# Four chained graph layers on one core: norms in two parts with pinned relus, another product order between two layers, and one turn moved to TensorE

## The chip, the core and the metric

The kernel runs on one core of a Trainium2 chip. The metric is the device time of one launch in microseconds (us). Before the change the median of three runs is 2624.2 us, the lowest 2624.03 and the highest 2625.35.

A core has engines that each work through a queue of their own: TensorE (PE, matrix products and 128x128 transposes, with weight loads PEld beside them), VectorE (DVE), ScalarE (ACT), GpSimd (POOL) and SyncE (SP, which here only issues DMAs). Engines wait for each other by semaphores. PSUM has eight banks, in which TensorE leaves its products and from which DVE and ACT fetch them ("evict").

## The reference, cut to what matters

`x` is 128 graphs of 128 nodes with 256 features. Four layers follow each other. Each begins with a layer norm without gain and a relu, and adds its result to `x`.

```python
# layer 0: three gates per node, two mixings by adj
h = relu(layernorm(x)); x = x + gated_mix(h, adj, edge_bias, ...)
# layer 1: attention of each graph within itself, masked
h = relu(layernorm(x)); x = x + (softmax(q k^T / 16 + adj, causal) v) Wo
# layer 2: three products, each followed by a mixing by A2 = adj * adj
h = relu(layernorm(x))
h = relu(A2 @ (h @ W1)); h = relu(A2 @ (h @ W2)); x = x + A2 @ (h @ W3)     # 256->512->1024->256
# layer 3: A_hat mixing, linear, batch norm over all nodes of all graphs, relu, linear, batch norm
h = relu(layernorm(x)); x = x + batchnorm(relu(batchnorm(A_hat @ h @ bW1.T + b1)) @ bW2.T + b2)
```

The layer norm needs the mean and the variance of each row of 256 numbers. The batch norms need the mean over everything, so the kernel has two passes: the first does all up to the first batch norm and writes `z` and `x` to DRAM, the second does the rest. All arithmetic is in float32.

## The kernel before

Four graphs make a group; there are 32. In the first pass a loop over groups `g` weaves four strands: layer 0 of group g+2 ("A"), the end of layer 1 and beginning of layer 2 of group g+1 ("B", then "b" for its successor), W2 and W3 of layer 2 for group g ("C"), layer 3 of group g-1 ("D", then "d"). Each strand is a Python generator. A string says which strand records its next piece:

```python
TURN = "CCBBCBCABCBBCABDBACBDDACDCADDCDCBDCADBCBACACbCBCBBCBBCBBCBCbBCd"
FINAL = "CCCCCCCCCCCCCCCCCCDCCCCDDdDDddDdDdDDdddd"      # last group
...
for k in TURN if g < LAST else FINAL:
    next(stream[k], None)
```

The layer norm of a group: statistics on DVE, four small operations on POOL, four relus on ACT with scale and bias.

```python
def norm(g, layer, bs=ALL, blocks=False):
    ...
    for k, b in enumerate(bs):
        nc.vector.bn_stats(st[:, k, :], xt[:, b, :])          # L366
    for k in range(n):
        nc.vector.bn_aggr(mv[:, k, :], st[:, k, :])           # L368
    ...
        nc.gpsimd.tensor_scalar(rs, mv[:, :, 1], LN_EPS, None, ALU.add)       # L372
        nc.gpsimd.tensor_tensor(rs, rs, nhalf[:, :n], ALU.pow)                # L373
        nc.gpsimd.tensor_scalar(sh, mv[:, :, 0], -1.0, None, ALU.mult)        # L374
        nc.gpsimd.tensor_tensor(sh, sh, rs, ALU.mult)                         # L375
    ...
        relu = nc.scalar.activation(                                          # L387
            dst, src, AF.Relu, bias=sh[:, k : k + 1], scale=rs[:, k : k + 1])
        if (g, layer) == (1, 0):
            tc.keep_in_program_order(relu)
    return h
```

`keep_in_program_order` pins an instruction: the recording layer may move others on their engine, not this one.

Layer 1 needs `h` transposed. The first group does it on TensorE (`turn`: eight 128x128 transposes into two PSUM banks, one evicted by ACT, one by DVE). The others send `h` to DRAM and back so that 32x32 blocks come to stand in their places (`swap`: four DMAs out, one back), and DVE turns the blocks (`cut`, L435):

```python
    h = norm(g, 1, bs, n == G)
    if n == G:
        blocks = h.rearrange("p b d -> p (b d)")
        swap(blocks, f"hc_{g}")
    yield
    hT = tile_of(g, bs, [P, DC, T], "dT", f"hT_{g}", 2)
    if n < G:
        turn(hT, h, bs, f"pt_{tail}")
    else:
        cut(hT.rearrange("p c t -> p (c t)"), blocks, DC * G)
```

The gate weights of layer 0 are made by twelve DVE operations `gs<-h,gw` (L558) of a group, a small sum `gl` and a sigmoid on ACT (`gt`, L566). With `gt`, ACT and DVE then make the matrices `m` (L577, L578, L585) and the bias (L589, L592); `m` goes through DRAM as `cc` and is turned by DVE (L435) before the products `pm<-h,m` (L610).

Products of 2x2 blocks are done in seven multiplications (`seven`, a Strassen-Winograd form): its pieces are called x, y, z (r = 0, 1, 4), then 5, 2, 6, 3. Between them ACT keeps copies (`p_t<-p_x`, L506) and DVE adds them.

```python
    px = bank(...); product(0, px, True);  t1 = kept(px, 1);             yield
    py = bank(...); product(1, py, True);  put((0, 0), py, t1);          yield
    pz = bank(...); product(4, pz, True);  t5 = kept(pz, 5);             yield
    product(5, px, False); t2 = kept(px, 2);                             yield
    product(2, pz, False); put((0, 1), pz, t2);                          yield
    product(6, px, False); put((1, 1), px, t5);                          yield
    product(3, px, False); put((1, 0), px, None);                        yield
```

In layer 2 the W2 products are two such sevens (`wide(0)`, `wide(1)`), and W3 is a third. The last `put` of `wide(q)` relus on ACT (L795) and makes four sums `h2s` on DVE (L457 to L460), which W3's third and later pieces read.

```python
    yield from wide(0)
    late = wide(1)
    for _ in range(6):
        yield next(late)
    third = seven(rows_by_half(h2s, SETS["3"], P), put_s, [P, 2, P], f"p3_{g}")
    yield next(third)           # W3's first piece
    yield from late             # then the seventh of the second W2
    yield from third
```

Meanwhile group g+1 begins its layer 2: norm, mixing `pm<-a2T,h` (L446), eviction `mT<-pm` on DVE and ACT (L449), sums `ms`, then the seven products `pu` with W1 (L474).

Of the kernel before, what the change touches and what calls it, by code (L numbers as in the profile page):

```python
# [15 lines left out]
P = 128  # L16
# [6 lines left out]
def kernel(  # L23
# [328 lines left out]
    def tile_of(g, bs, shape, tag, name, bufs):  # L352

        if len(bs) == G:
            return w.tile(shape, FP, tag=tag, name=name, bufs=bufs)
        if name not in whole:
            whole[name] = w.tile(shape, FP, tag=tag, name=name, bufs=bufs)
        return whole[name]

    def norm(g, layer, bs=ALL, blocks=False):  # L360

        xt, n, tail = X[g], len(bs), f"{layer}_{g}_{bs[0]}"
        st = small.tile([P, n, 6], FP, tag="st", name=f"st{tail}")
        mv = small.tile([P, n, 2], FP, tag="mv", name=f"mv{tail}")
# [4 lines that stand above are left out]
        rs = small.tile([P, n], FP, tag="rs", name=f"rs{tail}")  # L369
        sh = small.tile([P, n], FP, tag="sh", name=f"sh{tail}")  # L370
# [5 lines that stand above are left out]
        else:  # L376
            inv_sqrt(rs, mv[:, :, 1], LN_EPS)
            nc.vector.scalar_tensor_tensor(sh, mv[:, :, 0], -1.0, rs, ALU.mult, ALU.mult)
        h = tile_of(g, bs, [P, G, D], "h", f"h{layer}_{g}", 3)
        for k, b in enumerate(bs):  # L380
            dst, src = h[:, b, :], xt[:, b, :]
            if blocks:
                dst = h.rearrange("p b d -> p (b d)").rearrange(
                    "p (j k b r) -> p b j k r", j=P // 32, k=DC, b=G
                )[:, b]
                src = src.rearrange("p (k j r) -> p j k r", k=DC, j=P // 32)
            relu = nc.scalar.activation(  # L387
                dst, src, AF.Relu, bias=sh[:, k : k + 1], scale=rs[:, k : k + 1]
            )
            if (g, layer) == (1, 0):  # L390

                tc.keep_in_program_order(relu)
        return h

    def columns(dst, c, bs):

# [137 lines left out]
    def layer0(g, bs=ALL):  # L534

        xt, n, tail = X[g], len(bs), f"{g}_{bs[0]}"
        h = norm(g, 0, bs)
        yield
        gl = small.tile([P, n, 3], FP, tag="gl", name=f"gl_{tail}")
        gate_bias = gb[:, None, :].to_broadcast([P, n, 3])  # L540
        if g < 2:

            hT = tile_of(g, bs, [P, DC, T], "dT", f"h0T_{g}", 2)
            turn(hT, h, bs, f"ph_{tail}")
            yield
            pl = bank([P, n, 3], f"pl_{tail}")
            for k, b in enumerate(bs):
                for c in range(DC):
                    nc.tensor.matmul(
                        pl[:, k, :], hT[:, c, b * P : (b + 1) * P], gwT[:, c, :],  # L550
                        start=(c == 0), stop=(c == DC - 1),
                    )
            nc.vector.tensor_tensor(gl, pl, gate_bias, ALU.add)
        else:
            gs = w.tile([P, D], FP, tag="gs", name=f"gs_{tail}", bufs=1)
            for k, b in enumerate(bs):
                for i in range(3):
                    nc.vector.scalar_tensor_tensor(  # L558
                        gs, h[:, b, :], 1.0, gw[:, i, :], ALU.mult, ALU.mult,
                        accum_out=gl[:, k, i : i + 1],  # L560
                    )
                if k == n // 2 - 1:
                    yield
            nc.vector.tensor_tensor(gl, gl, gate_bias, ALU.add)
        gt = small.tile([P, n, 3], FP, tag="gt", name=f"gt_{tail}")
        nc.scalar.activation(gt, gl, AF.Sigmoid)  # L566
        yield


        um = tile_of(g, bs, [P, 2, G, D], "um", f"m_{g}", 1)  # L570
        bias = um[:, 0]
        cmb, cmbT = (
            um[:, 1, 2 * k : 2 * k + 2, :].rearrange("p a (b n) -> p (a b) n", n=P) for k in range(2)
        )
        flatT = cmbT.rearrange("p b n -> p (b n)")
        for k, b in enumerate(bs):
            nc.scalar.activation(cmb[:, b, :], ain, AF.Copy, scale=gt[:, k, 0:1])  # L577
            nc.vector.scalar_tensor_tensor(  # L578
                cmb[:, b, :], aout, gt[:, k, 1:2], cmb[:, b, :], ALU.mult, ALU.add
            )  # L580
            dst, one, now = cmb[:, b, :], ident, cmb[:, b, :]
            if g >= 2:
                dst = flatT.rearrange("p (j b r) -> p b j r", j=NQ, b=G)[:, b]
                one, now = (a.rearrange("p (j r) -> p j r", j=NQ) for a in (one, now))
            nc.vector.scalar_tensor_tensor(dst, one, gt[:, k, 2:3], now, ALU.mult, ALU.add)  # L585
        if g >= 2:
            swap(flatT, f"cc_{g}")
        for k, b in enumerate(bs):
            nc.scalar.activation(bias[:, b, :], eb, AF.Copy, scale=gt[:, k, 0:1])  # L589
        yield  # L590
        for k, b in enumerate(bs):
            nc.vector.scalar_tensor_tensor(  # L592
                bias[:, b, :], oeb, gt[:, k, 1:2], bias[:, b, :], ALU.mult, ALU.add
            )
        mine = slice(bs[0], bs[-1] + 1)
        if g >= 2:
            yield
            cut(cmb.rearrange("p b n -> p (b n)"), flatT, G)
            cmbT = cmb
        else:  # L600
            pc = bank([P, n, P], f"pc_{tail}")
            for k, b in enumerate(bs):
                nc.tensor.transpose(pc[:, k, :], cmb[:, b, :], ident)
            nc.vector.tensor_copy(cmbT[:, mine, :], pc)
        yield
        for q in range(bs[0] // 2, (bs[-1] + 1) // 2):
            pm = bank([P, 2, D], f"pm_{g}_{q}")
            for r in range(2):
                b = 2 * q + r
                nc.tensor.matmul(pm[:, r, :], cmbT[:, b, :], h[:, b, :], start=True, stop=True)  # L610
            half = slice(2 * q, 2 * q + 2)
            nc.vector.tensor_tensor(bias[:, half, :], pm, bias[:, half, :], ALU.add)
        yield
        nc.vector.scalar_tensor_tensor(
            xt[:, mine, :], bias[:, mine, :], 0.0, xt[:, mine, :], ALU.max, ALU.add
        )
        yield

    def layer1(g, bs=ALL):
# [1 line left out]

        xt, n, tail = X[g], len(bs), f"{g}_{bs[0]}"
        halves = range(bs[0] // 2, (bs[-1] + 1) // 2)
        h = norm(g, 1, bs, n == G)
        if n == G:
            blocks = h.rearrange("p b d -> p (b d)")
            swap(blocks, f"hc_{g}")
        yield
        hT = tile_of(g, bs, [P, DC, T], "dT", f"hT_{g}", 2)
        if n < G:  # L630
            turn(hT, h, bs, f"pt_{tail}")
        else:
            cut(hT.rearrange("p c t -> p (c t)"), blocks, DC * G)
            yield
            ex = w.tile([P, 4, 1, T // 2], FP, tag="ex", name=f"hs_{g}", bufs=2)
            hs = sums(nc.vector, quarters_t(hT), ex, ex[:, 3])
# [99 lines left out]
                    ALU.mult, ALU.add,  # L736
                )
        yield
        h = norm(g, 2, bs)
        yield  # L740
        mT = tile_of(g, bs, [P, DC, T], "dT", f"mT_{g}", 2)
        mixed(mT, h, a2T, f"pm2_{tail}", (nc.vector.tensor_copy, nc.scalar.copy), bs)
# [37 lines left out]
    def layer2(g):  # L780
# [39 lines left out]

        yield from wide(0)
        late = wide(1)
        for _ in range(6):
            yield next(late)
        third = seven(rows_by_half(h2s, SETS["3"], P), put_s, [P, 2, P], f"p3_{g}")
        yield next(third)
        yield from late
        yield from third
        for q in range(G // 2):
            pr = bank([P, 2, D], f"pr_{g}_{q}")  # L830
# [7 lines left out]
    def layer3(g):  # L838
# [1 line left out]

        parts = [ALL] if g < LAST else HALVES
        for bs in parts:
            h = norm(g, 3, bs)
            yield
        gT = tile_of(g, parts[0], [P, DC, T], "dT", f"gT_{g}", 2)
        for i, bs in enumerate(parts):
# [57 lines left out]

    TURN = "CCBBCBCABCBBCABDBACBDDACDCADDCDCBDCADBCBACACbCBCBBCBBCBBCBCbBCd"


    FINAL = "CCCCCCCCCCCCCCCCCCDCCCCDDdDDddDdDdDDdddd"  # L910
    US = {}
    AHEAD = 3

# [23 lines left out]
    for g in range(NG):  # L937
        if g + AHEAD < NG:
            load_x(g + AHEAD)
        if g == LAST:  # L940
            most1 = bn_part(stats1, FC, slice(LAST - 1), "most1")
        stream = {
            "A": part(layer0, g + 2), "B": bs, "C": layer2(g), "D": ds,
            "b": part(layer1, g + 2), "d": layer3(g),
        }
        for k in TURN if g < LAST else FINAL:
            next(stream[k], None)
        assert all(next(stream[k], k) == k for k in "ABCD")
        bs, ds = stream["b"], stream["d"]
# [243 lines left out]
```

## Time and profile before

| | |
|---|---|
| median of three runs | 2624.2 us |
| span of the profiled run | 2625.7 us |
| PE busy | 2524.2 us, 96% |
| DVE, ACT, POOL busy | 74%, 48%, 10% |
| stage 1000 to 1500 us (seven groups): PE busy | 489.93 of 500 us |
| stage 0 to 130 us: PE busy | 50.28 and 53.17 of two times 65 us |
| stage 2350 to 2550 us (second pass): PE busy | 199.9 of 200 us |

To read it: busy time is a share of the span, and PE's is a mean over three stages. The first 130 us prepare weights and fill the strands; from then to about 2300 us a group takes 71.6 us (in the timeline, the products `pmu` of one group begin at 1002.87 us and those of the next at 1074.51); the second pass follows. A time in square brackets in a timeline row is how long the engine sat idle before the row, and what ended the wait. A timeline's row shows a duration that overlaps the next row of the same engine a little: the distance between starts is the pace.

### The profile page before, as it was taken

To read this page: it belongs to the slowest core of one execution; us is meant where nothing else is said; L and a number is where in the kernel's file an instruction comes from. 1 tells how busy PE (TensorE), PEld (TensorE's weight loads), DVE (VectorE), ACT (ScalarE), POOL (GpSimd) and SP (SyncE) were. 2 spreads that over 40 slices of the span, in tenths; PEclk is the share of its full clock that TensorE was granted. 3 is DMA by queue.
4 is the path that set the end of the run, shared out by engine and by line. 5 is a ranking of instruction groups with operands and counts; after the bars stand their busy time and mean duration, and the time that the engine had idled before them with its cause. 6 is when DMAs were issued, how large, how long until landed. Compare 5 with 4: busy or idle time off the path is not lost.

```text
span 2625.7 us, 40828 instructions
## 1 busy us (share of the span) xinstructions
PE 2524.2 (96%) x14824; PEld 2255.9 (86%) x14824; DVE 1934.7 (74%) x4795; ACT 1248.9 (48%) x2546; POOL 269.1 (10%) x563
## 2 busy tenths in 40 slices
PE   7899999999999999999999999999999999999996
PEld 6788888888888888888888888888888888888885
DVE  7677777777777877777777777777777777548886
ACT  4444444444444444444444444444444444337766
POOL 1100111110011100111110011100111110000000
PEclk9899999999999999999999999999999999999998
DMA  4122211221121122211221221122112211026559
GB/s 132 48 64 65 57 46 60 65 65 57 57 65 56 58 65 65 57 46 60 65 65 57 58 65 57 57 65 65 50 52 61 65 57 55 26 83 229 176 183 386
DMA packets 115900, 207.59 MB, mean 79 GB/s; under 512 B 11618, under 2 KB 77684, under 8 KB 111732
## 3 DMA queue, kind: packets, MB, share of 16 engines
q1 hardware_dynamic: 109124, 181.85, 22.2%
q0 software_dynamic: 6432, 23.07, 2.5%
q8 instruction: 117, 1.92, 0.3%
q14 instruction: 83, 0.68, 0.1%
q10 hardware_dynamic: 144, 0.07, 0.0%
HBM read 105.72 MB, written 99.22 MB: 78 GB/s over the span
## 4 chain that ended last, share of the span: by engine, by line
PE 52%; DVE 21%; issue 11%; ACT 10%; POOL 4%; DMA 0%; SPq 0%; DVEq 0%; ACTq 0%; POOLq 0%
PE p_x L491 9%; PE p_x L474 7%; ACT h L387 5%; PE p_z L491 5%; PE pu_x L474 4%; PE pmu L446 4%; DVE gs L558 4%; PE pz_x L491 4%; DVE st L366 3%; PE p_z L474 2%; PE p_y L491 2%; DVE h2T L802 2%; POOL rs L373 2%; PE py L731 2%; PE ps L691 2%
## 5 line engine op out<-in xcount | busy, mean ns | idle before, releaser
L387 ACT ACTIVATE h<-x,sh,rs 128x256 f32<-128x256 f32 x512 | 269.2, 590 | 266.1 <-POOL sh L375 248.4
L491 PE MATMUL p_x<-uT,w 128*128 128x256 f32 x1024 | 247.5, 380 | 0.0
L803 ACT ACTIVATE h2T<-h2T 128x512 f32<-128x512 f32 x192 | 120.4, 627 | 223.8 <-DVE h2T L802 223.8
L506 ACT COPY p_t<-p_x 128x512 f32<-128x512 f32 (+1 forms) x192 | 96.1, 501 | 274.4 <-PE p_x L491 272.2
L491 PEld LDWEIGHTS p_x<-uT,w 128*128 128x128 f32 x1024 | 192.6, 191 | 38.3 <-issue 14.6
L558 DVE SCALAR_TENSOR_TENSOR gs<-h,gw 128x256 f32<-128x256 f32 x360 | 152.3, 423 | 79.6 <-ACT h L387 64.2
L366 DVE BATCH_NORM_STATS2 st<-x 128x6 f32<-128x256 f32 x512 | 182.5, 411 | 1.2
L372 POOL TENSOR_SCALAR rs<-mv 128x4 f32<-128x4 f32 x124 | 29.7, 240 | 1328.3 <-DVE mv L368 1275.6
L373 POOL TENSOR_TENSOR rs<-rs,nhalf 128x4 f32<-128x4 f32 x124 | 128.5, 1037 | 0.0
L491 PE MATMUL p_z<-us,w 128*128 128x256 f32 x512 | 125.3, 388 | 2.0 <-ACT p_t L506 1.9
L474 PEld LDWEIGHTS p_x<-w,h2T 128*128 128x128 f32 x1024 | 124.3, 192 | 3.3
L491 PE MATMUL p_z<-us,w_s 128*128 128x256 f32 x512 | 126.9, 382 | 0.0
L474 PE MATMUL p_x<-w,h2T 128*128 128x128 f32 x1024 | 124.6, 275 | 0.0
L491 PE MATMUL p_x<-uT,w_s 128*128 128x256 f32 x512 | 121.7, 380 | 1.3 <-DVE h2T L802 1.3
L491 PE MATMUL p_x<-us,w_s 128*128 128x256 f32 x512 | 121.0, 379 | 0.0
L491 PE MATMUL p_y<-uT,w 128*128 128x256 f32 x512 | 120.9, 379 | 0.0
L446 PE MATMUL pmu<-a2T,u 128*128 128x128 f32 x1024 | 119.6, 275 | 0.0
L446 PEld LDWEIGHTS pmu<-a2T,u 128*128 128x128 f32 x1024 | 116.9, 192 | 0.0
L449 DVE COPY uT<-pmu 128x512 f32<-128x512 f32 (+1 forms) x132 | 88.2, 672 | 36.6 <-PE pmu L446 36.4
L491 PEld LDWEIGHTS p_z<-us,w 128*128 128x128 f32 x512 | 95.2, 191 | 17.9 <-ACT p_t L506 2.6
L756 ACT ACTIVATE u<-u 128x512 f32<-128x512 f32 x93 | 58.6, 630 | 107.6 <-DVE u L755 106.5
L491 PEld LDWEIGHTS p_y<-uT,w 128*128 128x128 f32 x512 | 97.3, 190 | 13.2
(331 smaller groups left out, 6013.5 us busy)
## 6 DMA issues: line engine op xcount, KB each, us to landing
z<-zo SPq DMA_DIRECT2D x62, 512.0 KB, 2.6
zi<-z SPq DMA_DIRECT2D x31, 1024.0 KB, 4.9
x<-x POOLq DMA_DIRECT2D x32, 512.0 KB, 3.5
x<-in_x_dram SPq DMA_DIRECT2D x31, 512.0 KB, 3.9
hc<-h SPq DMA_DIRECT2D x124, 128.0 KB, 2.5
h<-hc SPq DMA_DIRECT2D x31, 512.0 KB, 3.5
out_dram<-x3i SPq DMA_DIRECT2D x30, 512.0 KB, 10.7
x3i<-x SPq DMA_DIRECT2D x20, 512.0 KB, 6.4
```

The lines of the kernel that those rows point to most:

```text
L366: nc.vector.bn_stats(st[:, k, :], xt[:, b, :])
L373: nc.gpsimd.tensor_tensor(rs, rs, nhalf[:, :n], ALU.pow)
L387: relu = nc.scalar.activation(dst, src, AF.Relu, bias=sh[:, k : k + 1], scale=rs[:, k : k + 1])
L446: nc.tensor.matmul(pm[:, k, :], src[:, b, c * P : (c + 1) * P], aT, start=True, stop=True)
L449: evicts[c % len(evicts)](columns(dst, c, bs), pm.rearrange("p b n -> p (b n)"))
L474: nc.tensor.matmul(pb[:, rr, :], a_r[r][:, c, rr * P : (rr + 1) * P], b_r[r][:, c, :wide], start=(first and rr == 0 and c == 0), stop=(c = ...
L491: nc.tensor.matmul(pb[:, jj, :], b_r[r][:, c, at : at + P], a_r[r][:, c, :], start=(first and jj == 0 and c == 0), stop=(c == nk - 1), ski ...
L506: nc.scalar.copy(t, pb)
L558: nc.vector.scalar_tensor_tensor(gs, h[:, b, :], 1.0, gw[:, i, :], ALU.mult, ALU.mult, accum_out=gl[:, k, i : i + 1],)
L691: nc.tensor.matmul(ps[:, k, :], qv[:, b // 2, c, 0, (b % 2) * P : (b % 2 + 1) * P], hT[:, c, b * P : (b + 1) * P], start=(c == 0), stop=(c ...
L756: nc.scalar.activation(dst, dst, AF.Relu)
L803: nc.scalar.activation(dst, dst, AF.Relu)
```

## The change

It has four parts.

1. `norm` is cut in two: the statistics and POOL's four operations are recorded by one step of the strand, the relus by the next. In groups of full size the relus are pinned to the place where they are recorded.
2. The strings of steps get the extra steps and another order (`TURN`, `FIRST` for group 0, `FINAL`).
3. In layer 2 the seventh product of the second W2 seven comes ahead of W3's first piece (not in the last group).
4. In group 1 layer 1 turns `h` on TensorE, as group 0 does, and not through DRAM.

What is computed stays the same.

```diff
-    def norm(g, layer, bs=ALL, blocks=False):
+    def norm(g, layer, bs=ALL):
...
+        def relus(blocks=False, pinned=False):
+            h = tile_of(g, bs, [P, G, D], "h", f"h{layer}_{g}", 3)
+            for k, b in enumerate(bs):
...
+                relu = nc.scalar.activation(
+                    dst, src, AF.Relu, bias=sh[:, k : k + 1], scale=rs[:, k : k + 1]
+                )
+                if pinned:
+                    tc.keep_in_program_order(relu)
+            return h
+        return relus
...
     def layer0(g, bs=ALL):
-        h = norm(g, 0, bs)
+        relus = norm(g, 0, bs)
+        if g >= 2:
+            yield
+        h = relus(pinned=g >= 1)
...
     def layer1(g, bs=ALL):
-        h = norm(g, 1, bs, n == G)
+        swapped = n == G and g >= 2
+        relus = norm(g, 1, bs)
         if n == G:
+            yield
+        h = relus(swapped, n == G)
+        if swapped:
             blocks = h.rearrange("p b d -> p (b d)")
             swap(blocks, f"hc_{g}")
         yield
         hT = tile_of(g, bs, [P, DC, T], "dT", f"hT_{g}", 2)
-        if n < G:
+        if swapped:
+            cut(hT.rearrange("p c t -> p (c t)"), blocks, DC * G)
+        else:
             turn(hT, h, bs, f"pt_{tail}")
-        else:
-            cut(hT.rearrange("p c t -> p (c t)"), blocks, DC * G)
+        if n == G:
             yield
...
-        h = norm(g, 2, bs)
+        relus = norm(g, 2, bs)
+        if n == G:
+            yield
+        h = relus(pinned=n == G)
...
         late = wide(1)
-        for _ in range(6):
+        for _ in range(6 if g == LAST else 7):
             yield next(late)
         third = seven(rows_by_half(h2s, SETS["3"], P), put_s, [P, 2, P], f"p3_{g}")
         yield next(third)
-        yield from late
+        yield from late if g == LAST else ()
         yield from third
...
-            h = norm(g, 3, bs)
+            relus = norm(g, 3, bs)
+            if g < LAST:
+                yield
+            h = relus(pinned=g < LAST)
...
-    TURN = "CCBBCBCABCBBCABDBACBDDACDCADDCDCBDCADBCBACACbCBCBBCBBCBBCBCbBCd"
-    FINAL = "CCCCCCCCCCCCCCCCCCDCCCCDDdDDddDdDdDDdddd"
+    TURN = "CCBBCBACDBCABBCABDBACBDDACDCADDCDCBDCADBCBACABCbCBbCBBCBBCBBCBCbBCd"
+    FIRST = "CCCB" + TURN[2:].replace("C", "", 1)
+    FINAL = "CCCCCCCCDCCCCCCCCCCDCCCCDDdDDddDdDdDDdddd"
...
-        for k in TURN if g < LAST else FINAL:
+        for k in FIRST if g == 0 else TURN if g < LAST else FINAL:
```

More of the change, by code (lines that the diff above doesn't have):

```diff
@@ L378, in norm @@
             nc.vector.scalar_tensor_tensor(sh, mv[:, :, 0], -1.0, rs, ALU.mult, ALU.mult)
[L379 to L393, printed above, removed]
+        def relus(blocks=False, pinned=False):
+            h = tile_of(g, bs, [P, G, D], "h", f"h{layer}_{g}", 3)
+            for k, b in enumerate(bs):
+                dst, src = h[:, b, :], xt[:, b, :]
+                if blocks:
+                    dst = h.rearrange("p b d -> p (b d)").rearrange(
+                        "p (j k b r) -> p b j k r", j=P // 32, k=DC, b=G
+                    )[:, b]
+                    src = src.rearrange("p (k j r) -> p j k r", k=DC, j=P // 32)
+                relu = nc.scalar.activation(
[5 more added lines that the diff above has]
+        return relus
     def columns(dst, c, bs):
```

## The prediction

> **What bounds the kernel now.** I read the page first, then the waits of PE, then the table of stages, then the timelines of one group. PE is busy 96% of the span, so only PE's idle time can be won, and its list of waits says where that lies (engine, line, waited for: us in total, times, longest):
>
> ```profile
> PE 2524.2 (96%) x14824; PEld 2255.9 (86%) x14824; DVE 1934.7 (74%) x4795; ACT 1248.9 (48%) x2546; POOL 269.1 (10%) x563
> ...
> PE pu_x L474 <- DVE mT L449: 34.8, 30, 1.2
> PE pqv_x L643 <- DVE hT L435: 8.6, 1, 8.6
> ...
> PE pqv_x L643 <- DVE qv L658: 6.1, 28, 0.4
> ...
> PE p_z L491 <- ACT p_t L506: 1.9, 1, 1.9
> ```
>
> The reader sees one wait that comes back in every group (34.8 us in 30 times) and two that come once. How the every-group wait arises is in the timelines of ACT, DVE and PE of one group (start, duration, engine, line, operation, idle before and what ended it):
>
> ```profile
> 1054.29 2.07 ACT L387 ACTIVATE h<-x,sh,rs 128x256 f32<-128x256 f32 x4 [3.45 <-POOL sh L375]
> ...
> 1056.52 0.59 ACT L795 ACTIVATE h2T<-p_x 128x512 f32<-128x512 f32 x1
> ```
> ```profile
> 1057.14 0.69 DVE L457 TENSOR_TENSOR h2s<-h2T 128x512 f32<-128x512 f32 x1 [1.83 <-ACT h2T L795]
> ...
> 1060.48 0.68 DVE L449 COPY mT<-pm 128x512 f32<-128x512 f32 x1
> ```
> ```profile
> 1061.21 1.13 PE L474 MATMUL pu_x<-w,mT 128*128 128x256 f32 x4 [1.17 <-DVE mT L449]
> ```
>
> The last product of the second W2 was finished at about 1054.5, but its relu (L795) stood behind four norm relus on ACT. DVE idled 1.83 us for it, then did four sums of 0.60 us and other things, and so evicted `mT` late; PE had been ready at 1059.88. The stall is 1.3 us.
>
> In group 1 the wait is a round trip through DRAM. The stages behind it (bounds, length, busy us of PE, PEld, DVE, ACT, POOL, PE clock, DMA share, GB/s) show what it costs beyond itself:
>
> ```profile
> 75.00:84.00 9.00, 0.43 (x3) 0.25 (x2) 7.97 (x32) 3.09 (x9) 0.00 (x0) 0.65 0.18 58
> 84.00:90.00 6.00, 6.00 (x24) 5.19 (x25) 3.93 (x12) 1.66 (x3) 0.00 (x0) 0.67 0.22 44
> ```
>
> PE was idle for 8.6 us and then worked 6 us at two thirds of its clock.
>
> **What the Trainium skill says.** "TensorE: Matmul & The Clock Gate", Part 1, says that PE's clock is halved after an idle window of about 3.4 us and needs about as long to return. The trace agrees for the long gap (clock 0.65 and 0.67, 1.00 before and after) and shows 1.00 through the 1.17 us gaps. The same section says that VectorE and ScalarE take their instructions in strict order; the ACT rows above agree: L795's input lay ready for 1.7 us while four norm relus, released late by POOL, stood ahead. So the order of instructions on ACT and DVE is what this change is about. "ScalarE: Activation LUTs", What ACT_TABLE_LOAD costs, gives about 1.28 us for a load; the trace has 1.28 for both of a group. "DMA: Bandwidth & Descriptors", Anatomy of one DMA, gives about 2 us of fixed time for a transfer; here `hc` lands 2.5 us after its issue and `h` 3.5.
>
> **The change part by part.** For the new places I read the order of the built program's instructions on each engine, which has no times, and walked through one group by hand with the trace's paces: DVE 0.60 us for 512 columns, 0.335 for 256, 0.47 for a gate operation with its accumulator, 0.33 for a statistic; ACT 0.47 for a copy, 0.49 for a norm relu; about 0.05 us from ACT or DVE to a waiting engine, 0.25 from the last matmul's end of pace; and 0.1 us more for the first matmul after any stall (1.13 against 1.03 in the rows of `pu_x`).
>
> *Group 1 by TensorE.* The eight transposes take 0.87 us of PE (eight like them, at 64.09, did). `h` is ready at 69.3 in the trace, so they don't wait; PE now has W2's z piece (1.73 us) ahead of them. ACT and DVE evict about 0.6 us each, and one matmul of 0.43 us fills, so `pqv_x` waits some 0.1 us and no longer 8.6. Won: 8.6 + 2.2 of slow clock (W2's z piece took 3.04 against 1.89, the two steps of `pqv_x` 1.19 and 1.06 against 0.59 and 0.61) - 0.9 - 0.1 = 9.8 us. But in group 0 the attention's own path (gates, softmax, its DMA) moves forward only some 7 us, by my walk, and PE will then wait 2 to 3 us for `p`. I keep **8 us**.
>
> *Last group.* The 1.9 us wait of `p_z` at 2305.85 came from four relus standing ahead of `p_t` on ACT; they now stand seven ACT operations later. After the gap the clock was 0.81: p_z took 3.07 against 1.89, and twelve matmuls 3.41 against 2.75. Won: 1.9 + 1.2 + 0.7 = **3.8 us**.
>
> *The middle, 30 groups.* Before, PE's stalls in a group are 1.3 at `pu_x`, and by differences of starts 0.4 and 0.2 and 0.1 and 0.1 at `pqv_x`, `pqv_z`, `p_z`, `py`: 2.1 us, and 0.4 of refill. After:
> - L795 now stands ahead of the norm relus, and the product it waits for comes 1.8 us sooner. `h2s` begins when DVE is free, not when ACT is. By the walk `mT` is ready 0.7 us before `pu_x` needs it: **the 1.3 us stall goes**.
> - The relus of layer 0's norm stand later (after one more copy and one relu). The twelve gate operations now begin 3.3 us later (21.58 against 18.28, from 1000) and are woven between evictions and sums; `gl` comes at 34.0, not 25.1. ACT then does sigmoid, table load, four exponentials (1.55), four copies into `m` (1.2) and four biases (1.6) ahead of `pz_t<-pz_z`, which is done at 41.07 where PE wants it at about 40.7: **a new stall of some 0.4**.
> - Everything behind it on DVE is in a row: statistics, turn of `p`, statistics, `h2T`, three of `x<-py`, and only then the turn of `m` (L435), which stood ahead of `x<-py` before:
>
> ```profile
> 1047.13 0.70 DVE L435 STREAM_TRANSPOSE m<-m 128x512 f32<-128x512 f32 x1
> 1047.75 1.61 DVE L734 SCALAR_TENSOR_TENSOR x<-py,rsum,x 128x256 f32<-128x256 f32 x4
> ```
>
>   In the walk `m` is turned at 50.1 and PE wants it for `pm<-h,m` at 49.4: **a new stall of some 0.7**, and 0.2 or 0.1 at `pqv_x`, `pz_x` and `py`.
>
> From `pm<-h,m` to `pu_x` no stall is left: 10.8 us against 11.9 in the trace. So `pu_x` starts at 1060.8, not at 1061.2: 0.4 us a group, 30 x 0.4 = **12 us**.
>
> Sum: 8 + 3.8 + 12 = 24; 2624.2 - 24 = 2600. The second pass (PE busy 199.9 of 200 us) is not touched.
>
> **The rivals.**
> 1. *The new stalls don't come.* My walk adds up some forty DVE steps; an error of 0.02 in each is as large as the stall at `m`. If gates and turn are in time, a group wins all but a few tenths of its 2.5 us, say 1.7: 51 + 12 = 63, 2561 us. For it: whoever set these strings placed relus one by one. Against it: the order on DVE is fixed and `m` stands behind three `x<-py` that need PE's own `py`.
> 2. *The wait moves and grows.* If the gates are later by another microsecond, the `cc` transfer (1.8 and 2.7 us to landing) comes on the path too: `m` is back at 46.8 in the walk, 2.6 us before its turn, so that much is spare. A group would lose 0.4: -12 + 12, 2624 us. For it: DVE has no idle time between 21.6 and 35.8 in the walk.
> 3. *The start gives nothing*, as group 0 to 2 are held by DMA and POOL anyway: 2608 us. For it: the stage 112 to 132 has waits for POOL (2.47 us). Against it: those lie behind the 8.6 us and move along with it.
>
> **Range and chances.** The start and end are worth 8 to 13. A group's gain is uncertain by 0.7 either way, 21 us over 30. That gives 2578 to 2618 for eight in ten. More than 2% faster, under 2571.7, needs 1.35 us or more a group: 0.09. More than 2% slower needs a loss of 2 us a group: 0.02.
>
> **What would show it.** PE's waits: `pu_x <- DVE mT` gone or under 5 us; `pqv_x <- DVE hT` gone; new rows `pm <- DVE m` of about 20 us in 30 times and `pz_z <- ACT pz_t` of about 10; a wait for `p` in group 0. Starts of `pmu` 71.2 us apart. `gt` about 9 us later in its group. Wrong would be: `pm` without a wait (then rival 1), or a group as long as before (rival 2).

## The result and the profile after

The changed kernel takes 2601.9 us (median of four runs, 2601.0 to 2602.7), the kernel before 2624.8 us beside it. The ratio is 0.991, with a 95% interval of 0.9893 to 0.9927: under 1% faster.

In the changed file the lines have moved. L389 is a norm relu (L387 before), L438 a turn by DVE (L435), L452 the eviction of a mixing (L449), L509 a kept copy (L506), L616 the product `pm<-h,m` (L610), L745 `x<-py` (L734), L809 the last W2 relu (L795), L477 the products with W1 and W2 (L474), L654 the product `pqv` (L643).

First the totals on the page of the kernel after, then its list of TensorE's waits (engine, line, waited for: us in total, times, longest):

```profile
PE 2520.7 (97%) x14832; PEld 2236.0 (86%) x14832; DVE 1921.9 (74%) x4795; ACT 1259.5 (48%) x2547; POOL 271.5 (10%) x563
```
```profile
PE pm L616 <- DVE m L438: 25.4, 30, 1.0
...
PE p_x L494 <- ACT p_t L509: 3.0, 1, 3.0
```

One wait in 30 groups has gone, the 34.8 us of `pu_x` for `mT`, and another in 30 groups has come, 25.4 us of `pm` for `m`. The single wait of `pqv_x` for `hT` (8.6 us) has gone, and a single one of 3.0 us for `p_t` has come. PE is busy for 2520.7 us (2524.2 before), so what shrank is almost all idle time: the span is 26.8 us shorter.

The stages of the kernel after, as before with PE, PEld, DVE, ACT and POOL in this order, then PE's clock, the DMA share and GB/s:

```profile
1000.00:1500.00 500.00, 493.71 (x2965) 439.73 (x2964) 374.33 (x966) 234.85 (x484) 57.08 (x124) 1.00 0.21 60
75.00:84.00 9.00, 9.00 (x54) 8.14 (x52) 4.26 (x15) 4.75 (x9) 0.00 (x0) 1.00 0.01 2
84.00:90.00 6.00, 6.00 (x40) 5.44 (x39) 5.83 (x23) 1.79 (x4) 0.00 (x0) 1.00 0.00 0
```

The stretch 75 to 90 us, in which PE stood still and then ran at two thirds of its clock, is now full at clock 1.00. In the stage of the groups PE is busy 493.71 of 500 us, before 489.93.

By the starts of the products `pmu`, which open a group's last mixing, the two profiled spans (2625.7 and 2598.9 us) come apart in four places:

| stretch | before | after | gained |
|---|---|---|---|
| to group 0's first `pmu` | 65.83 | 63.70 | 2.1 |
| from there to group 1's | 77.19 | 70.67 | 6.5 |
| 30 groups | 30 x 71.59 | 30 x 71.12 | 14.1 |
| the rest | 334.96 | 330.93 | 4.0 |

The 2.1 us are none of the change's: the first 60 us have the same instructions in the same order in both. In that launch the weights `w` landed 0.97 us earlier, and from 30 to 40 us TensorE's clock was 1.00 and not 0.83; in the other profiled runs the same place lies anywhere from 64.2 to 67.6 us. Without them the change is worth 24.6 us here, and 22.8 by the medians.

Now a group of the kernel after, by engine (start, duration, engine, line, operation, and in brackets the idle time before it and what ended it). ScalarE:

```profile
1019.15 0.21 ACT L572 ACTIVATE gt<-gl 128x12 f32<-128x12 f32 x1
...
1024.47 1.69 ACT L595 ACTIVATE m<-eb,gt 128x256 f32<-128x256 f32 x4
1026.07 0.56 ACT L509 COPY pz_t<-pz_z 128x512 f32<-128x512 f32 x1
...
1039.81 0.60 ACT L809 ACTIVATE h2T<-p_x 128x512 f32<-128x512 f32 x1 [2.25 <-PE p_x L494]
1041.02 2.08 ACT L389 ACTIVATE h<-x,sh,rs 128x256 f32<-128x256 f32 x4 [0.60 <-POOL sh L375]
```

L809 stands ahead of the four norm relus and waits for TensorE alone. That is the part of the change that worked as meant. VectorE and TensorE of the same group:

```profile
1033.97 1.35 DVE L745 SCALAR_TENSOR_TENSOR x<-py,rsum,x 128x256 f32<-128x256 f32 x3
1035.23 0.70 DVE L438 STREAM_TRANSPOSE m<-m 128x512 f32<-128x512 f32 x1
...
1045.16 0.68 DVE L452 COPY mT<-pm 128x512 f32<-128x512 f32 x1
```
```profile
1026.68 1.13 PE L494 MATMUL pz_z<-gs,bw1T 128*128 128x256 f32 x4
...
1034.63 0.59 PE L494 MATMUL p_x<-uT,w 128*128 128x256 f32 x2
1036.09 1.97 PE L616 MATMUL pm<-h,m 128*128 128x256 f32 x8 [0.86 <-DVE m L438]
...
1046.76 1.03 PE L477 MATMUL pu_x<-w,mT 128*128 128x256 f32 x4
```

`mT` is done at 1045.8, and `pu_x` starts at 1046.76 with nothing in brackets and in 1.03 us, not 1.13. From the start of `pm` to that of `pu_x` are 10.67 us, against 11.92 before. The time comes back ahead of `pm`: three `x<-py` stand in front of the turn of `m` on DVE, and TensorE is idle for 0.86 us.

### The profile page after: what moved, and what is told of

It is laid out like the page before. It is cut to its first block, busy times and chain, and to the rows that moved or that the text cites. A ratio compares the mean times of both kernels' runs of the same rounds, so it can differ in the third digit from the quotient of the medians.

```text
span 2598.9 us, 40812 instructions
## 1 busy us (share of the span) xinstructions
PE 2520.7 (97%) x14832; PEld 2236.0 (86%) x14832; DVE 1921.9 (74%) x4795; ACT 1259.5 (48%) x2547; POOL 271.5 (10%) x563
## 3 DMA queue, kind: packets, MB, share of 16 engines
q1 hardware_dynamic: 108404, 180.80, 22.3%
## 4 chain that ended last, share of the span: by engine, by line
PE 91%; DVE 4%; ACT 2%; DMA 1%; issue 1%; POOL 0%; SPq 0%; ACTq 0%; DVEq 0%; POOLq 0%
PE p_x L494 16%; PE p_x L477 9%; PE p_z L494 8%; PE pz_x L494 4%; PE p_z L477 4%; PE pmu L449 4%; PE p_y L494 4%; PE po_x L1084 4%; PE pu_x L477 4%; PE pz_z L494 2%; PE pm L616 2%; PE pm L449 2%; PE pqv_x L654 2%; PE pg L449 2%; PE p_y L477 2%; PE pr L845 2%
## 5 line engine op out<-in xcount | busy, mean ns | idle before, releaser
L389 ACT ACTIVATE h<-x,sh,rs 128x256 f32<-128x256 f32 x512 | 265.6, 589 | 69.9 <-POOL sh L375 57.8
L509 ACT COPY p_t<-p_x 128x512 f32<-128x512 f32 (+1 forms) x192 | 97.4, 507 | 299.4 <-PE p_x L494 291.2
L816 DVE TENSOR_TENSOR h2T<-p_z,p_t 128x512 f32<-128x512 f32 x64 | 43.6, 682 | 122.5 <-ACT h L389 108.3
L477 PEld LDWEIGHTS p_x<-w,h2T 128*128 128x128 f32 x1024 | 124.5, 192 | 3.3
L477 PE MATMUL p_x<-w,h2T 128*128 128x128 f32 x1024 | 124.8, 275 | 0.0
L494 PE MATMUL p_z<-us,w_s 128*128 128x256 f32 x512 | 121.0, 379 | 0.0
L449 PE MATMUL pmu<-a2T,u 128*128 128x128 f32 x1024 | 119.6, 275 | 0.0
L452 DVE COPY uT<-pmu 128x512 f32<-128x512 f32 (+1 forms) x132 | 88.4, 674 | 40.7 <-PE pmu L449 40.7
L449 PEld LDWEIGHTS pmu<-a2T,u 128*128 128x128 f32 x1024 | 116.9, 192 | 0.0
```

What stands on the lines that cost most here:

```text
L389: relu = nc.scalar.activation(dst, src, AF.Relu, bias=sh[:, k : k + 1], scale=rs[:, k : k + 1])
L449: nc.tensor.matmul(pm[:, k, :], src[:, b, c * P : (c + 1) * P], aT, start=True, stop=True)
L452: evicts[c % len(evicts)](columns(dst, c, bs), pm.rearrange("p b n -> p (b n)"))
L477: nc.tensor.matmul(pb[:, rr, :], a_r[r][:, c, rr * P : (rr + 1) * P], b_r[r][:, c, :wide], start=(first and rr == 0 and c == 0), stop=(c = ...
L494: nc.tensor.matmul(pb[:, jj, :], b_r[r][:, c, at : at + P], a_r[r][:, c, :], start=(first and jj == 0 and c == 0), stop=(c == nk - 1), ski ...
L509: nc.scalar.copy(t, pb)
```

## The experiments

All were timed beside the kernel before (medians 2625.25 to 2625.96 us). "After" is the changed kernel, 2601.9 us.

**turn_only: the kernel before with part 4 alone** (group 1 turned by TensorE).

```diff
-        h = norm(g, 1, bs, n == G)
+        swapped = n == G and g >= 2
+        h = norm(g, 1, bs, swapped)
...
-        if n < G:
-            turn(hT, h, bs, f"pt_{tail}")
-        else:
+        if swapped:
             cut(hT.rearrange("p c t -> p (c t)"), blocks, DC * G)
+        else:
+            turn(hT, h, bs, f"pt_{tail}")
```

> The kernel before with group 1's turn on TensorE and nothing else. My theory (the 8.6 us stall and the slow clock behind it go, some 2 us come back as a wait in group 0): about 8 us faster than before, 2616; PE's wait for hT gone, all 30 waits of pu_x for mT still there, groups 71.6 us apart. Rival (the start is held by DMA and POOL anyway): no gain, 2624.

Measured: 2616.5 us (2615.5 to 2619.9), ratio 0.9966 [0.9953, 0.9979], 8.8 us less than before. TensorE's waits:

```profile
PE pu_x L474 <- DVE mT L449: 34.9, 30, 1.2
```

The wait for `hT` is not in the list any more, and the one in every group is untouched; a group takes 71.60 us as before. So part 4 is worth about 9 us at the start and nothing later. The wait of some 2 us in group 0 that I expected back is not in the list.

**late7_only: the kernel before with part 3 alone** (seventh W2 product ahead of W3's first).

```diff
-        for _ in range(6):
+        for _ in range(6 if g == LAST else 7):
...
-        yield from late
+        yield from late if g == LAST else ()
```

> The kernel before with the seventh product of the second W2 ahead of W3's first and nothing else. On ACT the relu of that product still stands behind four norm relus; it only passes one small copy. My theory (what holds mT is the place of the norm relus on ACT, and the order of the products helps only with it): the stall at pu_x shrinks by 0.25 us a group, 7 us in all, about 2617. Rival (the order of the products is what counts): the stall of 1.3 us goes, 30 to 40 us faster, about 2588.

Measured: 2637.5 us (2636.8 to 2638.1), ratio 1.0042 [1.0027, 1.0057]. It is slower, and both expectations were wrong. ScalarE, VectorE and TensorE of one group:

```profile
1059.81 2.08 ACT L387 ACTIVATE h<-x,sh,rs 128x256 f32<-128x256 f32 x4 [3.45 <-POOL sh L375]
1061.79 0.57 ACT L795 ACTIVATE h2T<-p_x 128x512 f32<-128x512 f32 x1
```
```profile
1062.39 0.69 DVE L457 TENSOR_TENSOR h2s<-h2T 128x512 f32<-128x512 f32 x1 [2.22 <-ACT h2T L795]
...
1066.38 0.69 DVE L449 COPY mT<-pm 128x512 f32<-128x512 f32 x1
```
```profile
1067.12 1.13 PE L474 MATMUL pu_x<-w,mT 128*128 128x256 f32 x4 [1.56 <-DVE mT L449]
```

The product comes earlier, but its relu L795 still stands behind the four norm relus, so `h2T` is hardly earlier (0.24 us, counted from the group's `pmu`). What did change is DVE's order. Before, three of the next norm's four statistics were done in DVE's idle time ahead of `h2s`; now the sums are recorded ahead of them, and one is done in the idle time, three between `h2s` and `mT`. `h2s` to `mT` takes 3.99 us against 3.34. TensorE waits 1.56 us, and a group takes 72.00 us. I read this from the trace and did not undo the order of the statistics alone.

**after_late6: the kernel after with part 3 undone.**

```diff
-        for _ in range(6 if g == LAST else 7):
+        for _ in range(6):
...
-        yield from late if g == LAST else ()
+        yield from late
```

> The kernel after with W3's first piece ahead of the seventh product again. On ACT the product's relu then stands behind the four norm relus again. My theory: h2s begins 2 to 3 us later, mT is late for pu_x by about 1 us, and the groups are 0.9 us longer: 25 us slower than after, about 2627, no faster than before. Rival (the pinned relus alone bring the gain): within 8 us of after, about 2605.

Measured: 2624.3 us (twelve runs, 2622.2 to 2628.1), ratio 0.9998 [0.9989, 1.0006]: 22.3 us above the kernel after, and some 3 under what was expected. A group takes 71.84 us, more than the 71.59 of the kernel before; the time is no longer only because part 4 and the last group still gain. Its waits:

```profile
PE pm L616 <- DVE m L438: 25.7, 30, 1.3
PE pu_x L477 <- DVE mT L452: 13.4, 30, 0.9
```

The wait at `pm` is there in full, and that at `pu_x` comes back (13.4 us of the 34.8). So the two are separate, and part 3, which costs 12 us by itself, takes 22 us away where parts 1 and 2 surround it. Part 2, the strings, was not undone alone.

**after_no_pins: the kernel after, its relus recorded in the same places but not pinned** (save group 1's of layer 0, as before).

```diff
-                if pinned:
+                if (g, layer) == (1, 0):
```

> The kernel after without the pins, so that the recording layer puts the relus where it likes: those of layer 0 go forward, the gates come early as before, m is turned ahead of x<-py, and of the four relus of layer 2's norm two stand ahead of L809. My theory (the pins remove the small stalls at pqv but cost the waits at pz_z and pm): no wait of pm for m, the small waits at pqv_x back, a wait of pu_x for mT of some 0.3 us; 0.4 us a group better than after, about 2590. Rival (without pins the stall of pu_x comes back whole): 2612 or more.

Measured: 2606.8 us (2605.0 to 2608.9), ratio 0.9926 [0.991, 0.9943], between what was expected (2590) and the rival (2612 and above). Its waits, and ScalarE around L809:

```profile
PE pu_x L477 <- DVE mT L452: 25.5, 29, 0.9
PE pqv_x L654 <- DVE qv L669: 20.0, 28, 0.9
```
```profile
1040.43 1.09 ACT L389 ACTIVATE h<-x,sh,rs 128x256 f32<-128x256 f32 x2 [3.45 <-POOL sh L375]
1041.43 0.58 ACT L809 ACTIVATE h2T<-p_x 128x512 f32<-128x512 f32 x1
1041.91 1.09 ACT L389 ACTIVATE h<-x,sh,rs 128x256 f32<-128x256 f32 x2
```

The wait of `pm` is gone. Two that the kernel after does not have stand in its place. Free to move, two of layer 2's relus come ahead of L809, and `mT` is late again. And layer 0's relus come early enough that the gate operations run in one train on DVE, ahead of the sum `qv` that `pqv_x` waits for. That is as in the kernel before: in both `pqv_x` starts 23.6 us after `pmu`, and TensorE, which loses less ahead of it now, waits longer (0.70 us against 0.21). So some pins help and others cost.

**cut_first: the kernel after with `x<-py` made to follow the turn of `m` on DVE.** `follow` is the kernel's helper for an order between two instructions.

```diff
+            turned_m.append(nc.cur_bb.bb.instructions[-1].name)      # after the cut of m
...
+                if n == G and turned_m:                              # after each x<-py
+                    follow(nc.cur_bb.bb.instructions[-1], turned_m[-1])
```

> The kernel after with one order added on DVE: the four x<-py follow the turn of m. My theory (pm waits 0.86 us a group because the turn of m stands behind three x<-py): the wait of pm for m goes, and about 0.35 us comes back at pm<-a2T,h or pu_x, as x<-py ends 0.6 us later in PE's time; 0.6 us a group, 18 us faster than after, about 2584. Rival (m is not back from DRAM by then, or the chain through x<-py takes the place of the wait): no gain, 2602.

Measured: 2584.3 us (2583.3 to 2587.6), ratio 0.9843 [0.9828, 0.9858], and 2584 was expected. The stage:

```profile
1000.00:1500.00 500.00, 498.69 (x2996) 444.04 (x2996) 376.69 (x981) 235.95 (x488) 54.57 (x119) 1.00 0.21 60
```

The 30 waits of `pm` are gone; no other of their size took their place. Some 0.4 us a group comes back, as expected, but a little later: around the `pu_x` that reads `ms`. The run shows the cause of the waits: the gates are as late as in the kernel after (`gt` 30.4 us after `pmu` in both), so it is the three `x<-py` ahead of the turn. Nor is it the transfer of `cc`: in the kernel after `m` is back 44.8 to 45.3 us after `pmu` (in the seven groups whose landing the trace has), and the turn begins at 46.5. In cut_first it begins at about 45.0, and the transfer is next in line. VectorE's list of waits has a row that the kernel after lacks:

```profile
DVE m L439 <- DMA m<-cc: 1.7, 2, 1.4
```

**final_early: the kernel after, with group 30's relus of layer 3 again the first step of the last group.**

```diff
-    FINAL = "CCCCCCCCDCCCCCCCCCCDCCCCDDdDDddDdDdDDdddd"
+    FINAL = "DCCCCCCCCCCCCCCCCCCDCCCCDDdDDddDdDdDDdddd"
```

> The kernel after with the four relus of layer 3 of group 30 recorded first in the last turn, so that they stand behind the first copy on ACT, as before. My theory: PE's wait of 1.9 us for p_t comes back and 1.9 us of slow clock with it: 3.8 us slower than after, about 2606. Rival (the last group has slack elsewhere that hides this): 2602.

Measured: 2607.7 us (2604.5 to 2608.6), ratio 0.9926 [0.9909, 0.9943], 5.7 us above the kernel after. TensorE's row of `p_z` in the last group, first of the kernel after, then of this one:

```profile
2280.17 1.89 PE L494 MATMUL p_z<-us,w 128*128 128x256 f32 x8
```
```profile
2286.48 3.21 PE L494 MATMUL p_z<-us,w 128*128 128x256 f32 x8 [1.89 <-ACT p_t L509]
```

The wait of 1.89 us is back, and the row behind it takes 3.21 us where the other takes 1.89. In turn_only, where the last group is that of the kernel before, the wait is the same and the row is not slow:

```profile
2295.94 1.99 PE L491 MATMUL p_z<-us,w 128*128 128x256 f32 x8 [1.89 <-ACT p_t L506]
```

TensorE's clock over the first 3 us behind this wait was 0.60 in final_early and 0.63 in the kernel before, and 1.00 in turn_only and late7_only. So the wait is shown to come from the order, but the slow clock behind it comes in some launches and not in others. No run here shows what decides that.

**pins_layer2: the kernel after with pins only on layer 2's relus.**

```diff
-                if pinned:
+                if pinned and (layer in (2,) or (g, layer) == (1, 0)):
```

> The kernel after with pins for the relus of layer 2's norm alone (and, as before, for layer 0 of group 1). Against the kernel without pins only ACT's order changes in a group: L809 stands ahead of all four relus, not of two. My theory: the wait of pu_x for mT (0.85 us a group without pins) goes, no wait of pm for m comes, the wait at pqv_x of 0.7 us stays: 0.9 us a group less than without pins, about 2580. Rival (the pins of the other layers are what carries the gain of the change): 2602 or more.

Measured: 2571.2 us (2570.6 to 2573.4), ratio 0.9793 [0.9778, 0.9807], 30.7 us under the kernel after and 9 better than expected. A group takes 70.18 us. One steady wait is left:

```profile
PE pqv_x L654 <- DVE qv L669: 19.8, 28, 0.8
```

Layer 2's pins keep L809 ahead of the relus. Without those of layers 0, 1 and 3, `gt` comes 22.4 us after `pmu` as in the kernel before, not 30.4, and the turn of `m` is ahead of `x<-py` again. In the three runs with all pins and no added order (after, after_late6, final_early) `gt` is late and the turn stands behind `x<-py`; in all runs with `gt` at 22.4 to 22.9 it stands ahead. Which of the three layers' pins costs how much was not separated.

**pins_layer2_qv: the same, and strand B's piece that makes `qv` changes places with strand C's W2 piece ahead of it.**

```diff
-    TURN = "CCBBCBACDBCABBCABDBACBDD...
+    TURN = "CCBBCBACDBCABBBACDBACBDD...
```

> As pins_layer2, and in TURN the sixth piece of the qv products ahead of the sixth piece of the first W2 (CAB becomes BAC in three places that follow each other). On DVE qv<-pqv_x then stands ahead of h2T<-p_x and of one gate operation. My theory: the wait of 0.7 us at pqv_x goes too, 0.8 us a group with its refill, 20 to 24 us faster than pins_layer2, about 2557. Rival (PE waits for the copy pqv_t instead, or gt comes later and pz_z waits): 2575 or more.

Measured: 2548.5 us (2547.6 to 2550.5), ratio 0.9706 [0.9691, 0.972]. The stage:

```profile
1000.00:1500.00 500.00, 500.00 (x3024) 453.50 (x3023) 385.81 (x985) 236.16 (x492) 57.11 (x122) 1.00 0.22 64
```

The row shows no idle time of TensorE in the groups, each of which takes 69.41 us. That is 22.7 us less than pins_layer2, where 20 to 24 was expected. This version beats both kernels, that before by 2.8 to 3.1% and that after by 53 us.

**best_late6: that version with part 3 undone** (the edit of after_late6).

> The version with pins for layer 2's norm alone and qv ahead (2548.5 us, no steady wait), with part 3 of the change undone: W3's first product ahead of the seventh of W2 again, so that ScalarE's last W2 relu (L809) comes after the four relus of pu_x's norm as in the kernel before. Theory (part 3 is what lets TensorE go from pm to pu_x without a wait, whatever the pins are): h2T comes some 2 us later, the sums of h2 and mT with it, and pu_x waits for mT at 0.5 to 0.9 us in each of 30 groups: 15 to 27 us, so 2564 to 2576, and the row 'pu_x <- DVE mT' is back among TensorE's waits. Rival (with the pins gone from layers 0 and 1 DVE has less ahead of mT, and the order of the seventh product is worth nothing): 2546 to 2553 and no such row.

Measured: 2573.3 us (2572.2 to 2573.8), ratio 0.98 [0.9784, 0.9817], 24.8 us more than with part 3. Its waits begin with

```profile
PE pu_x L477 <- DVE mT L452: 15.8, 30, 0.9
```

So part 3 stays needed when most of the pins are gone.

## Why the prediction was right, point by point

The time was 2601.9 us where 2600 was predicted, and each term can be held against a run.

*Group 1 by TensorE, predicted 8.* Alone it gave 8.8 us by the medians. In turn_only's profile the stretch between the first two groups' `pmu` is 65.88 us, 11.3 under the kernel before; 9.8 was predicted ahead of what group 0 gives back. The 2 to 3 us that I took off for group 0 are not in that trace. In the kernel after the stretch shrank by 6.5 only. Of the 4.8 us between, 3.0 are a wait for another operand, `p_t`. ScalarE, then TensorE of the kernel after, then ScalarE of turn_only:

```profile
96.16 0.39 ACT L721 ACTIVATE pT<-p,nmax 128x128 f32<-128x128 f32 x1
...
96.55 0.56 ACT L509 COPY p_t<-p_x 128x512 f32<-128x512 f32 x1
```
```profile
97.16 1.99 PE L494 MATMUL p_x<-us,w_s 128*128 128x256 f32 x8 [2.98 <-ACT p_t L509]
```
```profile
94.20 0.58 ACT L506 COPY p_t<-p_x 128x512 f32<-128x512 f32 x1 [2.86 <-PE p_x L491]
94.80 1.28 ACT L712 ACT_TABLE_LOAD   x1
```

In the kernel after the copy that frees W2's bank stands behind biases, a table load and four exponentials of the attention; in turn_only it stands ahead of the load. The wait of 3.0 us is in the four runs with pins on all norms (after, after_late6, cut_first, final_early) and in none of the seven others. So it comes with those pins and not with part 4. Here the prediction named a wait that did not come and left out one of the same size that did: that 8 is near what came is in part luck.

*Last group, predicted 3.8.* The profile has 4.0 for all behind the last `pmu`, and `p_z` starts without a wait. Undoing that step alone cost 5.7 us by the medians, whose two ranges leave 1.8 to 7.6, and 3.8 by the profiles (334.7 against 330.9 us behind the last `pmu`). But 1.9 of the predicted 3.8 was slow clock, which turn_only and late7_only do not have behind the same wait. Their stretch behind the last `pmu` is 332.8 and 332.7 us, against 335.0 before. So the step is worth about 2 or about 4 us, by the launch, and the profile that the prediction was read from is of the second kind.

*The middle, predicted 0.4 us a group.* Measured 0.47. To see the parts I took in one group of each kernel the difference between TensorE's starts, less the pace of what was started (0.865 us for four 128x256 products, 1.785 for sixteen 128x128), and kept what is over 0.06.

| us lost in a group | before | after | pins_layer2_qv |
|---|---|---|---|
| `pu_x` and the row behind it | 1.44 | 0 | 0 |
| `pqv` and the products between | 0.99 | 0.29 | 0.10 |
| `pz_z`, `pz_x` and the `p_z` between | 0 | 0.62 | 0 |
| `py` | 0.18 | 0.18 | 0.18 |
| `pm<-h,m` | 0 | 1.10 | 0 |
| sum | 2.61 | 2.19 | 0.28 |

- The stall at `pu_x` went, as predicted.
- That at `pm` came: predicted 0.7, in the profile 0.86, and its row of waits has 25.4 us where about 20 was given. Its cause was named rightly, as cut_first shows. The late gates themselves (`gt` is 8.0 us later in its group, predicted about 9) cost nothing there: with the turn of `m` put ahead of `x<-py` on DVE the wait is gone. What the transfer of `cc` had to spare was 1.2 to 1.7 us, not 2.6.
- That at `pz_z` was too large in my sum: 0.18, not 0.4. It starts a train of five small delays, of which I had only `pz_x`. No row of `pz_z` in the list of waits answers to the 10 us predicted for it.
- The starts of `pmu` lie 71.12 us apart, predicted 71.2.

*The rivals.* The first (no new stalls, 2561) needed what the kernel did not have, the turn of `m` ahead of `x<-py`. With that order (cut_first) it took 2584, and with three layers' pins and the small delays gone 2549. The second, a group as long as before, did not come; it does without part 3 (after_late6, 2624), but by the stall at `pu_x` and not by this rival's transfer. The third, a start worth nothing, falls with turn_only.

*The range.* Its lower end, 2578, is the sum of its parts (13 at start and end, 33 in the groups). Its upper end is not: 8 at start and end and a loss of 9 in the groups make 2625, not 2618.

What I had not seen is how part 3 leans on the pins. I counted it as 1.8 us by which the product comes sooner; alone it loses 12 us. Its relu stands in the same place, so nothing is won, and the loss fits VectorE's new order in late7_only, which was read and not tested.

## What to carry to other kernels

When an engine takes its queue in order, look at what stands ahead of the instruction that the critical engine waits for, and move that: an early product cost 12 us with its eviction left in a late queue, and was worth 22 us once the eviction stood in front. Pin only what the path needs: the pins on one norm of four were worth 36 us (2571.2 against 2606.8 without any), and those on the other three cost 31 us, with these strings. One added order on VectorE wins 18 of the 31 back with all pins kept (cut_first, 2584.3). After each mended wait read the list of waits again, since the next one is already there.

## What was not expected

Busy time hid a part of the loss. This is the stage of pins_layer2; that of cut_first, with 498.69, stands above:

```profile
1000.00:1500.00 500.00, 495.09 (x3003) 448.57 (x3002) 383.25 (x981) 238.34 (x499) 56.12 (x119) 1.00 0.21 60
```

TensorE seems idler here, by 3.6 us in 500, and yet a group takes 70.18 us against 70.52. A row of four products is shown as 1.03 us long, with 0.865 to the next start, so a delay of up to 0.16 us lies inside the row and counts as busy. cut_first has several of these (the `pz` train of the kernel after, unchanged), pins_layer2 most of its loss in one wait of 0.70 us. The count of instructions in the stage (2996 and 3003) has the right order where the busy share has not, and the distance between two `pmu` is the safest.
